# LayerNorm statistics taken by bn_stats from the transposing blocks of x, score visits gathered, timetables made anew

## The chip, the cores and the metric

The kernel runs on one core of one Trainium2 chip, in one launch, all data float32. The metric is the device time of that core in microseconds (us). The engines are named as in the profile: PE is TensorE (PEld its weight loads), DVE is VectorE, ACT is ScalarE, POOL is GpSimd, and SP is SyncE, which issues nearly all transfers.

## The reference

One layer of graph attention with residual, on 128 graphs of 128 nodes and 768 features, with 12 heads of 64:

```python
h = jnp.maximum(_layernorm(x, axis=-1), 0.0)          # mean, variance over the 768 features
q, k, v = (split_heads(h @ W + b) for W, b in ((Wq, bq), (Wk, bk), (Wv, bv)))
scores = jnp.einsum('bhqd,bhkd->bhqk', q, k) / 8 + beta * adj[:, None]
scores = jnp.where(adj[:, None] > 0, scores, -9e15)
probs = softmax(scores, axis=-1)
out = x + merge_heads(jnp.einsum('bhqk,bhkd->bhqd', probs, v))
```

x is (128, 128, 768), adj is (128, 128, 128), the three weights are 768 x 768.

## The kernel before

**Groups and products.** The work goes in 32 groups of four graphs (`NG`, `GRP`). The three matrix products h·W of a group are made by a fast scheme for matrix multiplication with fewer products. A group has three slices: `qk0` (the first half of the columns of q and k), `v`, `qk1` (the other half). A slice is 15 products (`PRODUCTS`), each of a sum of blocks of h (`A00`... loaded, `S0`... made by `sum_acts`) with a prepared sum of blocks of the weights (`T..`, `B..`). A product is 7 zones of 128 columns, written as 28 matmul records in the trace; 45 products make a group, and "slot" counts them: the times in the tables below are in slots from the group's first product. Of the 45 prepared weights ten stay in SBUF (`RESIDENT`), 35 are loaded for each group by `load_T` (448 KB each) through a ring of six.

Products add up in four chains `a` to `d`. There are four pairs of PSUM banks; a chain takes a pair at its first product in a slice (`take`) and gives it back after its last. After every product its sum so far is added to one or two of the six results of its slice (`evict`): the first time a result is written ("opened") by ScalarE with a part on VectorE, later VectorE adds from PSUM, 128 x 896 elements at a time. **The chain's next product may start only after that eviction.** When a result has all its contributions, `decode` does four (q, k) or five (v) additions within it, most of them on GpSimd.

**Attention.** For each of the six head pairs oc = 0 to 5 of a group there follow, each an event of its own: `scores` on TensorE (two halves, from decoded q and k), `mask` (VectorE: cap, add the bias, PSUM to SBUF), `exp` (ScalarE), `attend` on TensorE, `drain` (ScalarE), `recip` (VectorE), `divide` (ScalarE), `add` to the residual x (VectorE, `xo`), `send`. Attends of a group are put between the zones of a product on TensorE. Each place in TensorE's order at which one or more scores stand in a row is called a visit below; an ordinary group has four: scores (0,2) and (0,1) together, (0,0) alone, (1,2) and (1,0) together, (1,1) alone.

**Layer norm.** The products need h transposed. x is loaded in blocks (`load_x`, tile `xp`: a partition has one quarter of the features, 192, of the nodes with one remainder by 32), normalised in place by ScalarE (`norm`: relu(x·rstd + shift), one call for each 192 of a partition), and transposed by VectorE (`to_hT`). In that layout a node's features lie on four partitions, in four quarters of the 128. Groups from 2 on therefore load x a second time by rows (`load_row`, partition = node, 384 KB for a graph); ScalarE sums a row and the squares of its deviations (`row_stats`); GpSimd makes rstd and shift (`powers`); two small transfers through DRAM turn them into the block layout (`turn_out`, `turn_in`).

**The order.** Everything is written out by hand-made times. `TABLE` has an entry for each event of an ordinary group in slots, `EVICT` the delay of each eviction behind its product, `DECODE` the delay and engine of each decode, `FIRST`, `SECOND`, `LAST` what differs at the first and last groups. `put` pushes all of it into one heap; `slice_z` issues a product and then all events whose time has come. Each engine runs its instructions in that order and waits where an input isn't there:

```python
        for k, n in enumerate(order):
            outs = product(G, sl, n)
            for i, f in enumerate(outs):
                put(base + k + EVICT.get((name, n, i), 0.5), f)
            ...
            while events and events[0][0] < base + k + 1:
                _, _, f, args = heapq.heappop(events)
                f(*args)
```

Group 0 is done without the fast scheme (`plain_slice`), while the weights are prepared; group 31 ends with halved scores and attends. If the masking's bounds fail on the data, a plain version (`general`) runs after; here it doesn't.

## Time and profile before

| | |
|---|---|
| median of 3 runs | 2664.78 us (2664.27 to 2664.83) |
| span of the profiled execution | 2664.1 us |
| PE busy | 2644.1 us, 99% |
| DVE / ACT / POOL busy | 2165.8 / 1755.1 / 2097.8 us (81 / 66 / 79%) |
| granted TensorE clock | 9 of 10 or more in all 40 slices |
| moved by transfers | 736.65 MB, mean 277 GB/s |
| an ordinary group (936.60 to 1017.66) | 81.06 us |
| the first planned group (122.10 to 206.90) | 84.80 us |

The profile is one execution by the hardware's profiler. Engine shares are averages over the whole span; the order of the work repeats with each group, so a group's stretch is read instead. An engine's wait is put down to the work that ended last before it. In rows of groups the columns are line, engine, operation, written tile, read tiles and shape, with the number of instructions, then busy us and mean ns of one, then the idle time before them. Timeline rows are start, duration (us), engine, line, operation.

### The profile page before, as it was taken

How to read it: one execution, taken by the hardware profiler on the slowest of the kernel's cores; microseconds unless marked ns; L12 is line 12 of the kernel's file. 1: busy time of each engine (PE TensorE's matmuls, PEld its weight loads, DVE VectorE, ACT ScalarE, POOL GpSimd, SP SyncE). 2: the span in 40 equal slices, each digit the busy share in tenths (PEclk: the TensorE clock that was granted, in tenths of full speed). 3: DMA queues.
4: the chain of work that ended last, by engine and by line, in shares of the span. 5: the costliest groups of instructions: out<-in, count | busy, mean ns of one | idle time of the engine just before them, and what ended most of it. 6: DMA issues, size and time to landing. Idle time of an engine off the chain costs nothing.

```text
span 2664.1 us, 121442 instructions
## 1 busy us (share of the span) xinstructions
PE 2644.1 (99%) x52041; PEld 2564.2 (96%) x52041; DVE 2165.8 (81%) x2702; ACT 1755.1 (66%) x4608; POOL 2097.8 (79%) x3043
## 2 busy tenths in 40 slices
PE   9999999999999999999999999999999999999998
PEld 8799999999999999999999999999999999999997
DVE  7878887878888788887788887888877888778876
ACT  2567766677666677666777666776667776667654
POOL 5877778877779777788777797777887777887774
PEclk9999999999999999999999999999999999999999
DMA  8899999998989999999999899999899898999885
GB/s 254 276 281 279 282 284 278 283 292 267 293 281 279 287 277 284 281 281 280 289 269 288 281 281 282 288 275 285 279 278 292 268 291 279 276 286 282 256 253 165
DMA packets 531572, 736.65 MB, mean 277 GB/s; under 512 B 106444, under 2 KB 371160, under 8 KB 531032
## 3 DMA queue, kind: packets, MB, share of 16 engines
q1 hardware_dynamic: 530384, 728.06, 88.5%
q8 instruction: 411, 6.73, 1.0%
q14 instruction: 129, 1.06, 0.1%
q10 hardware_dynamic: 648, 0.79, 0.1%
HBM read 662.22 MB, written 66.51 MB: 274 GB/s over the span
## 4 chain that ended last, share of the span: by engine, by line
PE 94%; DVE 1%; DMA 0%; issue 0%; ACT 0%; SPq 0%; DVEq 0%; ACTq 0%
PE pair L681 80%; PE pair L776 7%; PE pair L855 6%; PE pair L1048 1%; DVE home L704 0%; DMA x<-in_x_dram 0%; DMA T_qk<-kept_qk 0%; PE pair L926 0%; DVE e L789 0%; DVE prep_qk L403 0%; ACT e L836 0%; DVE res_qk L403 0%; PE pair L947 0%; DVE e L931 0%; ACT e L933 0%
## 5 line engine op out<-in xcount | busy, mean ns | idle before, releaser
L704 DVE TENSOR_TENSOR home<-home,pair 128x896 f32<-128x896 f32 x836 | 880.0, 1077 | 220.5 <-PE pair L681 179.8
L681 PE MATMUL pair<-sbig,T_qk 128*64 128x128 f32 x13020 | 827.6, 274 | 2.3 <-DVE home L704 1.2
L681 PEld LDWEIGHTS pair<-sbig,T_qk 128*64 128x64 f32 x13020 | 702.5, 137 | 19.9 <-issue 12.1
L739 POOL TENSOR_TENSOR home<-home 128x256 f32<-128x256 f32 x308 | 266.1, 864 | 320.0 <-DVE home L704 319.7
L681 PE MATMUL pair<-T_v,sbig 128*64 128x128 f32 x7812 | 457.8, 273 | 1.6 <-ACT home L716 0.6
L681 PE MATMUL pair<-A,T_qk 128*64 128x128 f32 x6944 | 445.6, 273 | 0.9 <-issue 0.9
L681 PEld LDWEIGHTS pair<-T_v,sbig 128*64 128x64 f32 x7812 | 430.7, 137 | 8.4 <-ACT e L836 4.8
L855 PE MATMUL pair<-v,e 128*64 128x65 f32 x6048 | 403.5, 221 | 0.0
L836 ACT ACTIVATE e<-e,sm 128x64 f32<-128x64 f32 x1512 | 381.7, 341 | 7.4 <-DVE sm L824 6.1
L681 PEld LDWEIGHTS pair<-A,T_qk 128*64 128x64 f32 x6944 | 384.6, 137 | 1.5 <-issue 1.5
L855 PEld LDWEIGHTS pair<-v,e 128*64 128x64 f32 x6048 | 362.2, 137 | 3.2
L724 ACT ACTIVATE home<-pair 128x640 f32<-128x640 f32 x340 | 240.6, 708 | 188.5 <-PE pair L681 187.2
L681 PE MATMUL pair<-sbig,res_qk 128*64 128x128 f32 x4340 | 312.3, 273 | 0.4
L742 POOL TENSOR_TENSOR home<-home 128x256 f32<-128x256 f32 x308 | 269.7, 876 | 24.1
L885 ACT ACTIVATE sm<-pair,tiny 128x8 f32<-128x8 f32 x189 | 50.8, 269 | 329.5 <-PE pair L855 329.5
L789 DVE SCALAR_TENSOR_TENSOR e<-pair,biasT 128x1024 f32<-128x1024 f32 x189 | 229.4, 1214 | 34.1 <-PE pair L776 33.0
L740 POOL TENSOR_TENSOR home<-home 128x256 f32<-128x256 f32 x308 | 228.2, 741 | 24.1
L681 PEld LDWEIGHTS pair<-sbig,res_qk 128*64 128x64 f32 x4340 | 238.0, 137 | 1.4 <-DVE home L704 1.3
L560 ACT ACTIVATE x<-x,block 128x192 f32<-128x192 f32 x480 | 222.6, 540 | 0.0
L726 ACT ACTIVATE home<-pair,bqk 128x128 f32<-128x128 f32 x680 | 214.3, 377 | 0.0
L798 ACT ACTIVATE e<-e 128x1024 f32<-128x1024 f32 x189 | 196.1, 1055 | 21.8 <-DVE e L789 14.0
L741 POOL TENSOR_TENSOR home<-home 128x128 f32<-128x128 f32 x308 | 175.6, 570 | 24.2
(208 smaller groups left out, 4401.6 us busy)
## 6 DMA issues: line engine op xcount, KB each, us to landing
T_qk<-kept_qk SPq DMA_DIRECT2D x713, 448.0 KB
T_v<-kept_v SPq DMA_DIRECT2D x372, 448.0 KB
xo<-in_x_dram SPq DMA_DIRECT2D x190, 256.0 KB
out_dram<-xo SPq DMA_DIRECT2D x189, 256.0 KB
x<-in_x_dram SPq DMA_DIRECT2D x248, 192.0 KB
sbig<-in_x_dram SPq DMA_DIRECT2D x116, 384.0 KB
kept_qk<-prep_qk SPq DMA_DIRECT2D x23, 448.0 KB
adj<-in_adj_dram SPq DMA_DIRECT2D x128, 64.0 KB
```

The source lines that it names most:

```text
L560: nc.scalar.activation(t, t, AF.Relu, bias=shift[G, n], scale=rstd[G, n])
L681: nc.tensor.matmul(p[q:q + HD, at, :], lhs[:, q:q + HD], rhs, start=(first and at % 4 == 0), stop=True, skip_group_check=True)
L704: nc.vector.tensor_tensor(t, t, p[:, 0:7], op)
L724: nc.scalar.activation(t[:, 0:5], p[:, 0:5], AF.Copy, scale=float(sign))
L726: nc.scalar.activation(t[:, at], p[:, at], AF.Identity, bias=bqk[:, of, oc:oc + 1], scale=float(sign))
L739: e.tensor_tensor(t[:, 1:4:2], t[:, 1:4:2], twice(5), ALU.add)
L740: e.tensor_tensor(t[:, 2:5:2], t[:, 2:5:2], twice(1), ALU.add)
L742: e.tensor_tensor(t[:, 0:7:6], t[:, 0:7:6], twice(2), ALU.add)
L789: nc.vector.scalar_tensor_tensor(e[:, :, at], ps[:, :, at], SCORE_CAP * ISCALE, bias[:, :, at], op0=ALU.min, op1=ALU.add)
L798: nc.scalar.activation(e, e, AF.Exp, scale=1.0 / ISCALE)
L836: nc.scalar.activation(o[:, r, b, 0:HD], pa[:, r, b, 0:HD], AF.Copy, scale=t[:, 1, r, b:b + 1])
L855: nc.tensor.matmul(pa[q:q + HD, 2 * g + i, :], k[:, q:q + HD], vt[G, "v", r, h // 4][:, 4 * g + h % 4, :], start=True, stop=True, skip_gro ...
```

## The change

**Statistics.** From group 2 on, `load_row`, `row_stats`, `moments`, `turn_out` and `turn_in` are gone. In their place, for each half r of a group (two graphs): `bn` makes eight `bn_stats` of 128 x 192 on VectorE from the blocks that `load_x` brought; `stout` writes their 48 numbers of each partition to DRAM (192 bytes each), `stin` reads them back so that every partition has those of all four quarters (768 bytes each); `comb` joins the quarters in six small VectorE operations; `powers` makes rstd and shift in three on GpSimd.

**Order.** The product orders `ORDER`, the resident set, `TABLE`, `EVICT` and `DECODE` are new. The scores (0,2), (0,1), (0,0) stand in a row at slot 18.86, (1,2) and (1,0) at 49.99, (1,1) at 56.3: three visits a group. The program as a whole has 128 visits before and 99 now (before 67 single and 61 double; now 38 single, 32 double, 29 triple), with the same scores. Attends 1, 3 and 5 are issued whole, the others still between a product's zones (`WHOLE`). Groups 1, 2 and 31 have times of their own (`OVER`), group 0's preparation a table (`EARLY`).

**Engines.** The adds of oc 0, 1, 4, 5 and the sums S11, S10, S2 go to GpSimd (`ADD_POOL`, `SUM_POOL`); the decodes of qk0 (1,1), v (1,0) and v (1,1) come to VectorE, beside that of qk1 (0,0), which is there before too. `OPEN` lists first evictions that VectorE takes wholly (2) or for three of seven zones (1). `did` and `needs` are assertions while the program is built and issue nothing.

TensorE where the first scores of a group stand (pair is a PSUM pair, home and sbig hold results of products; L776 is a score, L681 a product). Before, two visits:

```order
L776 MATMUL pair_73<-home_154 64x128 x8
L776 MATMUL pair_73<-home_148 64x128 x8
L776 MATMUL pair_76<-home_153 64x128 x8
L776 MATMUL pair_76<-home_150 64x128 x8
L681 MATMUL pair_75<-T_v_12918,sbig 64x128 x14
L681 MATMUL pair_74<-T_v_12982,sbig 64x128 x14
L681 MATMUL pair_73<-T_v_13047,sbig 64x128 x14
L681 MATMUL pair_75<-res_v_105,A_10_11668 64x128 x14
L681 MATMUL pair_73<-T_v_13078,sbig 64x128 x14
L681 MATMUL pair_74<-T_v_13096,sbig 64x128 x14
L776 MATMUL pair_76<-home_155 64x128 x8
L776 MATMUL pair_76<-home_151 64x128 x8
```

Now (L910 is a score, L805 a product), one visit:

```order
L805 MATMUL pair_76<-T_v_14367,sbig 64x128 x14
L910 MATMUL pair_73<-home_148 64x128 x8
L910 MATMUL pair_73<-home_151 64x128 x8
L910 MATMUL pair_74<-home_154 64x128 x8
L910 MATMUL pair_74<-sbig 64x128 x8
L910 MATMUL pair_75<-home_149 64x128 x8
L910 MATMUL pair_75<-home_153 64x128 x8
L805 MATMUL pair_76<-T_v_14385,sbig 64x128 x14
```

The third score of the slice, six products later before, stands with the other two, and three PSUM pairs are filled in a row.

VectorE at the turn from one group to the next (L704 and L829 are accumulating evictions, L739 to L742 and L871 to L874 a decode, L585 and L697 sums of blocks of h, L904 and L1050 adds, L789 a mask). Before:

```order
L704 TENSOR_TENSOR sbig<-sbig,pair_76 128x896
L739 TENSOR_TENSOR home_154<-home_154 128x2x128
L740 TENSOR_TENSOR home_154<-home_154 128x2x128
L741 TENSOR_TENSOR home_154<-home_154 128x128
L742 TENSOR_TENSOR home_154<-home_154 128x2x128
L585 TENSOR_TENSOR sbig<-sbig 128x896
L904 TENSOR_TENSOR xo_1_15013<-xo_1_15013,e_1_14509 128x512
L789 SCALAR_TENSOR_TENSOR e_5_15231<-pair_74,biasT_13463 128x1024
```

Now:

```order
L829 TENSOR_TENSOR home_148<-home_148,pair_73 128x896
L871 TENSOR_TENSOR home_148<-home_148 128x2x128
L872 TENSOR_TENSOR home_148<-home_148 128x2x128
L873 TENSOR_TENSOR home_148<-home_148 128x128
L874 TENSOR_TENSOR home_148<-home_148 128x2x128
L630 TENSOR_REDUCE total_0_14041<-sbig 128x8
L631 TENSOR_SCALAR total_0_14041<-total_0_14041 128x8
L632 TENSOR_TENSOR sbig<-sbig,total_0_14041 128x64
L633 TENSOR_TENSOR sbig<-sbig 128x64
L634 SCALAR_TENSOR_TENSOR sbig<-sbig 128x64
L635 TENSOR_REDUCE total_0_14041<-sbig 128x8
L1050 TENSOR_TENSOR xo_2_13632<-xo_2_13632,e_2_13421 128x512
L697 TENSOR_TENSOR sbig<-sbig,A_11_13039 128x896
```

Between the decode and the first sum (S6 now, S0 before) stand the six operations of comb 0 and an add. On TensorE the first products of the new group stand so, and the last of these rows is the product of S6:

```order
L805 MATMUL pair_73<-A_10_11758,T_qk_12_13868 64x128 x14
L805 MATMUL pair_76<-A_11_13702,res_qk_4_102 64x128 x14
L805 MATMUL pair_75<-sbig,T_qk_1_13893 64x128 x14
L999 MATMUL pair_74<-v_101,e_1_13441 64x65 x8
L999 MATMUL pair_74<-v_96,e_1_13441 64x65 x8
L805 MATMUL pair_73<-sbig,T_qk_0_13919 64x128 x14
L805 MATMUL pair_76<-A_11_13744,T_qk_8_13955 64x128 x14
L805 MATMUL pair_75<-sbig,T_qk_5_13978 64x128 x14
```

The first row is the old group's last product; the two L999 rows are attend 1, whole, and before it no attend stood there.

The diff, cut to its core:

```diff
-ORDER = {"qk0": (1, 0, 5, 2, 10, 3, 6, 7, 13, 11, 9, 4, 14, 12, 8), "v": (1, 0, 5, 2, 10, 3, 6, 7, 13, 11, 4, 9, 14, 8, 12), "qk1": (4, 1, 0, 8, 2, 5, 3, 6, 7, 10, 9, 13, 11, 12, 14)}
+ORDER = {'qk0': (4, 1, 0, 8, 5, 2, 3, 10, 6, 7, 13, 9, 11, 12, 14), 'v': (4, 1, 8, 5, 10, 0, 3, 2, 7, 13, 6, 11, 9, 14, 12), 'qk1': (4, 3, 0, 8, 1, 7, 2, 5, 11, 6, 10, 14, 9, 13, 12)}
-RESIDENT = (10, 12, 16, 21, 29, 33, 36, 39, 41, 42)
+RESIDENT = (0, 7, 8, 9, 12, 17, 21, 30, 33, 35)
...
-    (5.399, 'sum', 'S5'), (8.41, 'sum', 'S14'), (9.857, 'sum', 'S11'), (17.129, 'scores', 0, 2),
-    (17.594, 'mask', 2), (18.011, 'exp', 2), (17.884, 'scores', 0, 1), (20.163, 'mask', 1),
+    (5.640192, 'sum', 'S5'), (9.325594, 'sum', 'S14'), (9.958879, 'sum', 'S11'), (18.858473, 'scores', 0, 2),
+    (18.861473, 'scores', 0, 1), (18.864473, 'scores', 0, 0), (19.806037, 'mask', 2), (20.078002, 'exp', 2),
...
+ADD_POOL = (0, 1, 4, 5)
+SUM_POOL = ('S11', 'S10', 'S2')
+WHOLE = (1, 3, 5)
...
+    def bn(G, g):
+        for b in range(NB):
+            nc.vector.bn_stats(st_x[:, (g % 2) * NB + b, :], xg[G, g][:, b, :])
+
+    def stout(G, r):
+        t = turned[G, r] = dram.tile([SQ, NB, 2 * NB * 6], F32, name=f"turned_{G}_{r}")
+        nc.sync.dma_start(t.rearrange("i a s -> a i s"), st_x.rearrange("p m s -> p (m s)"))
+
+    def stin(G, r):
+        nc.sync.dma_start(back.rearrange("p a m s -> p (a m s)"), turned.pop((G, r)).rearrange(
+            "i a s -> i (a s)")[None].to_broadcast([NB, SQ, NB * 2 * NB * 6]))
+
+    def comb(G, r):
+        v = back.rearrange("p a m (h s) -> p a m h s", h=2)
+        total = stat.tile([P, 2, 2 * NB], F32, tag="total", name=f"total_{G}_{r}", bufs=1)
+        nc.vector.tensor_reduce(total[:, 0], v[:, :, :, :, 1].rearrange("p a m h -> p m a h"), AX.XY, ALU.add)
+        nc.vector.tensor_scalar(total[:, 0], total[:, 0], -0.125, None, op0=ALU.mult)
+        nc.vector.tensor_tensor(dev, v[:, :, :, :, 1], total[:, 0][:, None, :, None].to_broadcast([P, NB, 2 * NB, 2]), ALU.add)
+        nc.vector.tensor_tensor(dev, dev, dev, ALU.mult)
+        nc.vector.scalar_tensor_tensor(dev, v[:, :, :, :, 2], 2.0 / QD, dev, op0=ALU.mult, op1=ALU.add)
+        nc.vector.tensor_reduce(total[:, 1], dev.rearrange("p a m h -> p m a h"), AX.XY, ALU.add)
...
-    def load_row(G, g):
-        nc.sync.dma_start(row_at(G, g), x[G * GRP + g])
-
-    def row_stats(G, g):
-        nc.scalar.activation(row, row, AF.Copy, accum_out=s[:, 0, g:g + 1])
-        nc.scalar.mul(s[:, 1, g:g + 1], s[:, 0, g:g + 1], -1.0 / D)
-        nc.scalar.activation(row, row, AF.Square, bias=s[:, 1, g:g + 1], accum_out=s[:, 2, g:g + 1])
...
+        e = nc.gpsimd if name in SUM_POOL and G > 1 else nc.vector
+        e.tensor_tensor(t, full[G, a], full[G, b], ALU.add if sign > 0 else ALU.subtract)
...
+        if (G or oc > 2) and oc in WHOLE:
+            for _ in steps:
+                pass
+        else:
+            between.append(steps)
...
-        e = nc.gpsimd if G == NG - 1 and oc < 3 else nc.vector
+        e = nc.gpsimd if oc in ADD_POOL and 0 < G < NG - 1 or G == NG - 1 and oc < 3 else nc.vector
```

More of the change, by code (lines that the diff above doesn't have):

```diff
@@ L292, in load_x @@
             home_x(G, r)
+        if G > 1:
+            for k in range(3):
+                needs("turn", *((G, f"A0{k}") if r else (1, f"A0{k}") if G == 2 else (G - 1, f"A1{k}")))
+        for _ in parts:
+            did("x", G, r)
         src = x[G * GRP + 2 * r:G * GRP + 2 * r + 2].rearrange("g (b i) (a f) -> a i (g b) f", i=SQ, a=NB)
@@ L670, in product @@
             banks[chain] = take()
+        needs("A", G, an)
+        assert not waiting.get(chain)
+        waiting[chain] = len(uses)
         bank = banks[chain]
@@ L769, in scores @@
         oc = 3 * u + j
+        if G:
+            needs("decode", G, u, j, n=2)
         ps = take()
```

443 lines of the change are left out of this document (263 added, 180 removed), and 71 rows, old and new, of tables (DECODE, EVICT, OPEN, TABLE).

## The prediction

> **What bounds the kernel now.** I read the page's head and its chain, then the stretches of a steady group, then what TensorE waited for, then its timeline around the score visits.
>
> ```profile
> span 2664.1 us, 121442 instructions
> PE 2644.1 (99%) x52041; PEld 2564.2 (96%) x52041; DVE 2165.8 (81%) x2702; ACT 1755.1 (66%) x4608; POOL 2097.8 (79%) x3043
> PE 94%; DVE 1%; DMA 0%; issue 0%; ACT 0%; SPq 0%; DVEq 0%; ACTq 0%
> ```
>
> TensorE is busy 99% of the span and is 94% of the chain that ended last. So work saved on another engine shortens nothing by itself: only TensorE's own time, or its waits, can. The profiled span is 0.7 us below the median of the runs (2664.78); I sum against 2664.1 and add 0.7 at the end.
>
> The stretches (us, busy time and count of PE, PEld, DVE, ACT, POOL, clock, DMA share, GB/s) are one steady group, and the first planned one:
>
> ```profile
> 936.60:1017.66 81.06, 81.06 (x1650) 79.45 (x1646) 66.57 (x79) 55.62 (x146) 65.48 (x95) 1.00 0.91 283
> 122.10:206.90 84.80, 81.92 (x1646) 79.37 (x1644) 67.22 (x80) 59.20 (x160) 61.50 (x89) 1.00 0.92 284
> ```
>
> A steady group is 81.06 us without an idle microsecond on TensorE, at clock 1.00. VectorE has 14.5 us to spare in it, ScalarE 25, GpSimd 15.6. What TensorE waited for (us, times, longest):
>
> ```profile
> PE pair L681 <- issue: 2.4, 6, 1.1
> PE pair L681 <- DVE home L704: 2.2, 2, 1.2
> PE pair L1048 <- ACT home L1065: 1.2, 1, 1.2
> PE pair L681 <- ACT home L716: 0.8, 2, 0.6
> PE pair L681 <- DVE e L789: 0.5, 1, 0.5
> ```
>
> These five are 7.1 us, all that new timetables could win back from waits at products. None of them is a wait for a transfer, so the second load of x is paid for nowhere on TensorE.
>
> **The change, part by part.** First TensorE. The counts of products, scores and attends stay; only the places of the scores move. Its timeline (start, length):
>
> ```profile
> 941.32 1.98 PE L776 MATMUL pair<-home 64*64 64x128 f32 x64
> ...
> 947.86 1.70 PE L681 MATMUL pair<-A,T_qk 128*64 128x128 f32 x28
> 949.49 1.10 PE L776 MATMUL pair<-home 64*64 64x128 f32 x32
> 950.52 1.97 PE L681 MATMUL pair<-sbig,T_qk 128*64 128x128 f32 x32
> ...
> 954.56 1.70 PE L681 MATMUL pair<-A,T_qk 128*64 128x128 f32 x28
> ...
> 968.66 1.70 PE L681 MATMUL pair<-T_v,sbig 128*64 128x128 f32 x28
> 970.28 1.98 PE L776 MATMUL pair<-home 64*64 64x128 f32 x64
> 972.19 4.04 PE L681 MATMUL pair<-T_v,sbig 128*64 128x128 f32 x70
> 1016.04 6.40 PE L681 MATMUL pair<-sbig,T_qk 128*64 128x128 f32 x112
> 1022.38 1.98 PE L776 MATMUL pair<-home 64*64 64x128 f32 x64
> ```
>
> The last row's start is 81.06 after the first's: the group's period. Four products from 1016.04 take 6.12 without their tail, 1.53 each. From the start of a product to the next one with one score between are 950.52 − 947.86 = 2.66, so the single visit costs 1.13; with two scores 972.19 − 968.66 = 3.53, a visit of 2.00. The second score adds 0.87; a visit has 0.26 beyond its scores. From 950.52 to 954.56 lie two products and an attend: 4.04 − 3.06 = 0.98 for the attend. The program has 128 visits before and 99 after, so **29 × 0.26 = 7.5 us** go. A triple visit isn't in the trace: if its switches cost again at each score the saving is 0, if they cost once it is 7.5. The double visit costs one 0.26, not two, so I take 7.5. Of the 7.1 us of waits I take half, **3.5**: new timetables are made for the early groups, where these waits can lie, but they move them rather than remove what causes them.
>
> Then what leaves: four row loads a group and their statistics on ScalarE.
>
> ```profile
> sbig<-in_x_dram SPq DMA_DIRECT2D x116, 384.0 KB
> SPq L543 <- DMA turned<-row: 4.2, 8, 1.0
> ```
>
> 116 × 384 KB are 45.6 MB, 1.57 a group against some 22.9 (81.06 us at 283 GB/s): the DMA share falls from 0.91 to about 0.84. Worth nothing on TensorE, since nothing waits there. Two small transfers out and two in replace one of each; the queue's wait before the one back has been at most 1.0 us, and the stream of prepared weights behind it runs six products ahead, 9 us. I cost it at nothing; were the ring empty it would be 1.0 a transfer.
>
> What arrives lands on VectorE:
>
> ```profile
> L464 DVE BATCH_NORM_STATS2 st<-x 128x6 f32<-128x192 f32 x16 | 4.4, 343 | 2.6 <-DMA x<-in_x_dram 2.6
> 67.83 0.15 DVE L478 TENSOR_REDUCE mean<-pair 128x16 f32<-128x32 f32 x1
> 68.25 0.27 DVE L481 TENSOR_TENSOR dev<-dev 128x32 f32<-128x32 f32 x1
> L904 DVE TENSOR_TENSOR xo<-xo,e x186: 674/715/1270, 126.2 to 2612.7; 128x512 f32<-128x512 f32 x186
> L904 DVE TENSOR_TENSOR xo<-xo,e 128x512 f32<-128x512 f32 x186 | 161.8, 870 | 0.1
> L585 DVE TENSOR_TENSOR sbig<-A,A 128x896 f32<-128x896 f32 x93 | 114.1, 1227 | 3.3 <-POOL A L592 3.3
> L711 DVE TENSOR_TENSOR home<-bv_b,pair 128x256 f32<-128x256 f32 x171 | 71.7, 420 | 122.1 <-PE pair L681 111.3 <-POOL home L741 7.6 <-ACT sbig L521 2.0
> L904 POOL TENSOR_TENSOR xo<-xo,e 128x512 f32<-128x512 f32 x3 | 3.6, 1185 | 9.1 <-ACT e L836 9.1
> L977 DVE TENSOR_TENSOR xo<-xo,o_last x1: 426/426/426, 2658.7 to 2658.7; 128x256 f32<-128x256 f32 x1
> L975 DVE TENSOR_TENSOR xo<-xo,o_last x3: 281/281/282, 2657.0 to 2660.3; 128x128 f32<-128x128 f32 x3
> ```
>
> Sixteen bn_stats of 0.343 are 5.5. Two combs of six small operations, each between 0.15 and 0.27, are 1.8 to 3.2; I take 2.5. Three more decodes: one is three operations of 128x256 and one of 128x128, at best 3 × 0.426 + 0.281 = 1.56, and at worst the 3.12 shown below, so 4.7 to 9.4. First evictions taken over from ScalarE (896, 640 and 384 columns, one each a group) are 2.4 by the 0.420 of 256 columns scaled up and the accumulating eviction's 1.0. Four adds leave (4 × 0.87 = 3.5) and three sums (3 × 1.23 = 3.7). From 66.6 this makes 66.6 + 5.5 + 2.5 + 2.4 − 3.5 − 3.7 + (4.7 to 9.4) = **74.5 to 79.2** in a period of 80.8. VectorE's spare time falls from 14.5 to between 1.6 and 6.3. GpSimd: 65.5 + 4 adds × 1.2 + 3 sums × 2.1 (1.185 × 896 / 512) − 3 decodes × 2.9 (below) = 67.9 and some small powers; ScalarE falls.
>
> That alone costs nothing; it costs where a result is due. The tightest place I find is the **turn from one group to the next**, where VectorE now does this:
>
> ```profile
> 1017.84 1.09 DVE L704 TENSOR_TENSOR sbig<-sbig,pair 128x896 f32<-128x896 f32 x1 [0.25 <-PE pair L681]
> 1018.84 0.65 DVE L739 TENSOR_TENSOR home<-home 128x256 f32<-128x256 f32 x1
> ...
> 1021.96 1.34 DVE L585 TENSOR_TENSOR sbig<-sbig 128x896 f32<-128x896 f32 x1
> ```
>
> The last product of the old group ends at 1016.04 + 1.53 = 1017.57; its eviction starts 0.27 later and holds VectorE 1.00, the decode 3.12 (1018.84 to 1021.96), the sum 1.34. The sum is ready at 1023.30. Its product, the fifth of the new group, comes after three products (to 1022.16), the double visit and a fourth, at 1022.16 + 2.00 + 1.53 = 1025.7: 2.4 us to spare. After the change the fifth product needs the sum S6, behind four products and an attend: 4 × 1.53 + 0.98 = 7.1 us after the old group's end. VectorE reaches S6's end after the eviction, the decode, comb 0 and an add: 0.27 + 1.00 + 3.12 + 1.25 + (0.67 to 1.27) + (1.16 to 1.27) = 7.5 to 8.2 if the decode runs as now, 5.9 to 6.6 if it runs at 1.56. So S6 lies between 0.5 early and 1.1 late, a wait of 0 to 1.1 a group. I take 0.15, between on time and the 0.3 or so of the row it is nearest to (now's decode with the short add, 7.5, less the 0.1 by which consecutive operations overlap): **29 × 0.15 = 4.4**. Behind comb 0 stand the add, S6 and S0, then the evictions of the first two products.
>
> On the price of that decode: beside the quickest add, 0.674, stand adds up to 1.270, for one shape; the excess is what meeting GpSimd's work costs. The Trainium skill, "SBUF — State Buffer", section "SBUF: two separate sides", says that a VectorE operation with two SBUF inputs and a GpSimd operation that reads SBUF exclude each other for a whole instruction, the loser blocking fully. By that the new long GpSimd operations would cost VectorE more than the rows' excess of 0.6; that is the case of blocked ports below.
>
> **Sum.** 2664.1 − 7.5 − 3.5 + 4.4 = 2657.5; with 0.7, **2658 us**.
>
> **Rivals.** *VectorE late at the turn* (slower). Decodes on VectorE stay slow and S6 comes 0.8 late in each group: 2657.5 − 4.4 + 29 × 0.8 = 2676.3, so 2677. It decides once VectorE's row of work at the turn is longer than 7.1 us by more than the visit saves, 0.26. For it: 7.5 to 8.2 above, and a second such place where the v decode now on VectorE precedes an eviction that frees a chain. Against: the adds' median of 0.715 lies near their quickest, so meetings with GpSimd are the exception.
>
> *The triple visit waits for GpSimd.* Scores stand in TensorE's order, so one late decode holds everything.
>
> ```profile
> 1012.93 1.58 POOL L739 TENSOR_TENSOR home<-home 128x256 f32<-128x256 f32 x1
> ...
> 1017.14 0.72 POOL L739 TENSOR_TENSOR home<-home 128x256 f32<-128x256 f32 x1
> ...
> 1019.29 0.79 POOL L742 TENSOR_TENSOR home<-home 128x256 f32<-128x256 f32 x1
> ```
>
> A decode takes GpSimd 2.9 (1017.14 to 1020.08) to 4.2 (1012.93 to 1017.14). From the product that completes the first of three decodes which it needs, the thirteenth of the group, to its third score are six products, three attends and two scores with their visit, 9.2 + 2.9 + 2.0 = 14.1; GpSimd must in that time wait 1.3 for the eviction and do three decodes and a 2.1 us sum: 12.1 with quick decodes, 13.4 with one slow, 16.0 with three. At 0.3 a group in place of the turn's wait: 2657.5 − 4.4 + 8.7 = 2661.8, so 2662.
>
> *Blocked ports* (slower).
>
> ```profile
> L704 DVE TENSOR_TENSOR home<-home,pair x836: 1027/1081/1091, 133.6 to 2648.4; 128x896 f32<-128x896 f32 x168
> ```
>
> If each of GpSimd's three sums of 2.1 us holds up a VectorE operation by half its length, VectorE loses 3.2 a group against 1.6 to 6.3 spare; at a wait of 0.6 a group 2657.5 − 4.4 + 17.4 = 2670.5, so 2671. Against it: the evictions, most of VectorE's work, show no spread at all (1027 to 1091), whatever GpSimd does.
>
> *The merged visit saves nothing*: 2664.
>
> **How the numbers follow.** Forecast 0.50, late turn 0.21, late triple visit 0.15, blocked ports 0.07, no saving 0.07. The forecast's own range goes from 2650 (all waits won back, none new) to 2661 (S6 0.25 late). The range is 2647 to 2678: it holds the forecast, the triple visit, blocked ports and no saving, and the lesser half of the late turn (2677 is its middle); below it would lie gains that no row shows. A measurement here tells apart about 0.2%, 5.3 us: below 2659.4 is faster, above 2670.1 slower. Faster: 0.45 of the forecast and 0.05 of the triple visit, 0.50. Same: the forecast's rest 0.05, triple visit 0.08, no saving 0.07, a short late turn 0.03, 0.23. Slower: late turn 0.18, ports 0.07, triple visit 0.02, 0.27.
>
> **What would show it.** The period from one triple visit to the next: 80.8 without waits, 80.95 as forecast, above 81.06 if the rivals hold. The triple visit 0.26 + 3 × 0.87 = 2.87 on TensorE. TensorE's waits: products for a sum would be the late turn, scores for a GpSimd decode the late triple visit, products for evictions VectorE full at another place. VectorE busy 75 to 79 a group, DMA share 0.84. The mean of the qk decode's operations on VectorE says whether 1.56 or 3.12 holds. The forecast is wrong if the waits exceed 0.26 a group, or if bn_stats costs well above 0.343 on these tiles.

## The result: 20324 us, and what the profile after shows

| | before | after |
|---|---|---|
| median, runs of one chip | 2664.81 us (2664.27 to 2665.88) | **20324.06 us** (20315.26 to 20335.22) |
| ratio | | 7.625 (7.614 to 7.636) |
| span of the profiled execution | 2664.1 us | 20313.5 us |
| of it, until the flag of the masking's bounds is made | all | 2708.7 us |

The forecast of 2658 us was wrong twice. The program does nearly all its work a second time, in its plain version; and the first pass, the work that was forecast, isn't 6 us shorter but 44.6 us longer. The page of the kernel after (busy time; the granted clock and the moved GB/s in 40 slices of the span):

```profile
PE 10549.6 (52%) x91977; PEld 9041.3 (45%) x91977; DVE 6526.6 (32%) x18408; ACT 4176.2 (21%) x13928; POOL 2889.5 (14%) x5260
PEclk9999976666666666666666666666666666666666
GB/s 253 262 262 262 259 92 26 26 26 27 26 28 26 26 26 27 28 26 26 26 26 26 27 27 26 26 26 26 28 26 26 26 26 26 28 27 26 26 26 26
```

Only the first five slices (508 us each) look like the kernel before. The timeline at the change-over:

```profile
2708.14 0.31 PE L1506 MATMUL pair<-over,ones 128*1 128x89 f32 x2 [3.56 <-DVE over L1116]
2708.50 0.23 DVE L1507 TENSOR_REDUCE bad<-pair 1x1 int32<-1x89 f32 x1
2709.55 0.20 POOL masks.py:197 MEMSET g_ident<- 128x128 f32 x1 [8.23 <-DVE bad L1507]
```

`bad` collects whether a sum of exponentials left its bounds. With it set, `general` starts: every later instruction works on tiles named `g_`. That is 17.6 ms.

**Why the flag is set** is read in the code, and the first experiment bears it out. `st_x`, into which `bn` writes, lies inside the tile that still holds x of group 1's second half. For group 2 the table of exceptions has

```python
    (2, 'bn', 1): 37.0592, ...      # in OVER
    (37.1557, 'turn', 1, 'A11'), ...
```

so `bn` of group 2's second graph writes its 24 numbers a partition just before `A11` of group 1 is transposed out of the same columns. One graph of group 1 then gets columns of sums in place of normalised x, and the flag rises. `stin` asserts that the turns `A1k` have been; `bn` does not.

**The first pass.** Two groups of the kernel after, a steady one and the first planned one (us, then PE, PEld, DVE, ACT, POOL, clock, DMA share, GB/s), and what TensorE waited for until 2710:

```profile
952.10:1034.70 82.60, 81.21 (x1649) 79.55 (x1647) 74.14 (x117) 45.46 (x125) 69.27 (x92) 1.00 0.90 262
121.40:210.20 88.80, 84.18 (x1647) 81.17 (x1644) 75.44 (x118) 47.80 (x134) 64.08 (x91) 0.98 0.83 251
```

```profile
PE pair L805 <- ACT home L856: 18.1, 28, 0.7
PE pair L805 <- issue: 10.4, 14, 1.8
PE pair L805 <- ACT home L842: 9.6, 9, 2.7
```

A steady group takes 82.60 against 81.06 before, the first 88.80 against 84.80. TensorE's waits come in three kinds, each with its place.

The forecast's own two places first, in the timeline of that steady group (the group begins at 952.12):

```profile
953.46 0.81 DVE L871 TENSOR_TENSOR home<-home 128x256 f32<-128x256 f32 x1
...
955.97 0.27 DVE L630 TENSOR_REDUCE total<-sbig 128x8 f32<-128x64 f32 x1
...
957.29 0.22 DVE L635 TENSOR_REDUCE total<-sbig 128x8 f32<-128x64 f32 x1
...
957.43 0.68 DVE L1050 TENSOR_TENSOR xo<-xo,e 128x512 f32<-128x512 f32 x1
...
958.03 1.08 DVE L697 TENSOR_TENSOR sbig<-sbig,A 128x896 f32<-128x896 f32 x1
958.25 2.36 POOL L647 TENSOR_TENSOR rstd<-total,nhalf 128x8 f32<-128x8 f32 x1
...
959.21 1.75 PE L805 MATMUL pair<-sbig,T_qk 128*64 128x128 f32 x28
...
960.93 2.74 ACT L661 ACTIVATE x<-x,shift,rstd 128x192 f32<-128x192 f32 x6 [2.93 <-POOL shift L648]
...
963.58 2.01 ACT L974 ACTIVATE e<-e,sm 128x64 f32<-128x64 f32 x8
...
966.07 0.61 ACT L856 ACTIVATE home<-pair,bqk 128x128 f32<-128x128 f32 x2
...
966.73 1.75 PE L805 MATMUL pair<-sbig,res_qk 128*64 128x128 f32 x28 [0.66 <-ACT home L856]
```

The decode is 2.51 (953.46 to 955.97), comb 1.5 (to 957.51), the sum S6 is ready at 959.11 and its product starts at 959.21: on time. What is late stands 7 us further on: comb, the power on GpSimd (2.36 for 128 x 8 numbers), six norms on ScalarE, a divide, and only then the first eviction (L856) for which the next product of chain a waits, 0.66 here. This is the 18.1 us row.

```profile
987.64 1.70 PE L805 MATMUL pair<-T_v,sbig 128*64 128x128 f32 x28
989.27 1.54 PE L910 MATMUL pair<-home 64*64 64x128 f32 x48
990.63 0.62 PE L910 MATMUL pair<-sbig 64*64 64x128 f32 x16
991.07 1.05 PE L910 MATMUL pair<-home 64*64 64x128 f32 x32
992.05 1.20 PE L805 MATMUL pair<-T_v,sbig 128*64 128x128 f32 x18
```

The triple visit: product to product 992.05 − 987.64 = 4.41, less 1.53 for the product, is 2.88. The forecast said 2.87.

The row of 9.6 us (`ACT home L842`), at its longest, further on in the kernel after. SPq issues transfers, L606 is bn, L837 an eviction's part on VectorE, L841 and L842 the rest of it on ScalarE:

```profile
2217.68 5.72 SPq L533 DMA_DIRECT2D T_v<-kept_v  x4
...
2220.82 0.42 DVE L837 TENSOR_TENSOR home<-bv_b,pair 128x256 f32<-128x256 f32 x1 [0.51 <-PE pair L805]
...
2224.50 1.14 DVE L606 BATCH_NORM_STATS2 sbig<-x 128x6 f32<-128x192 f32 x4 [3.26 <-DMA x<-in_x_dram]
...
2225.55 0.73 DVE L837 TENSOR_TENSOR home<-bv_b,pair 128x256 f32<-128x256 f32 x2
2225.99 0.60 ACT L841 ACTIVATE home<-pair 128x512 f32<-128x512 f32 x1 [3.95 <-DVE home L837]
...
2226.48 0.27 ACT L842 ACTIVATE home<-pair 128x128 f32<-128x128 f32 x1
...
2226.80 1.52 PE L805 MATMUL pair<-res_v,A 128*64 128x128 f32 x22 [2.71 <-ACT home L842]
```

Read from the bottom: the product waits 2.71 for ScalarE, which waits 3.95 for VectorE, which has stood 3.26 at its first bn because x hadn't landed. Everything queued behind bn on VectorE stands with it. At all 9 places of this row, a bn that had itself waited at least 0.25 us stands in the 6 us before. Over the steady groups (busy, mean ns, then the idle time before bn; and what SyncE's queue waited for):

```profile
L606 DVE BATCH_NORM_STATS2 sbig<-x 128x6 f32<-128x192 f32 x456 | 126.5, 342 | 32.2 <-DMA x<-in_x_dram 24.0 <-DMA T_qk<-kept_qk 4.4 <-DMA T_v<-kept_v 2.0
```

```profile
SPq L620 <- DMA turned<-sbig: 94.4, 53, 3.2
SPq L612 <- DVE sbig L606: 73.4, 28, 4.4
```

The third kind, `issue`, is TensorE waiting for nothing the profile names. In the trace's transfer records most of them end 1.3 to 1.7 us after a packet of 16 KB has landed on the queue marked "instruction" (q8): some 15 us at 18 places of the first pass, worked out from the starts of TensorE's instructions, against some 3 us at 8 places before. That is a coincidence in time; that TensorE waits for what the packet holds is not shown.

### The profile page after: what moved, and what is told of

It reads as the page before. It is cut to its first block, busy times and chain, and to the rows that moved or that the text cites. A ratio compares the mean times of both kernels' runs of the same rounds, so it can differ in the third digit from the quotient of the medians.

```text
span 20313.5 us, 288774 instructions
## 1 busy us (share of the span) xinstructions
PE 10549.6 (52%) x91977; PEld 9041.3 (45%) x91977; DVE 6526.6 (32%) x18408; ACT 4176.2 (21%) x13928; POOL 2889.5 (14%) x5260
## 5 line engine op out<-in xcount | busy, mean ns | idle before, releaser
L1571 PE MATMUL g_pt<-g_ident,g_xn 128*128 128x128 f32 x4608 | 1977.9, 429 | 7923.1 <-DVE g_xn L1567 7640.8
L1571 PEld LDWEIGHTS g_pt<-g_ident,g_xn 128*128 128x128 f32 x4608 | 919.4, 200 | 8462.4 <-issue 7752.4
L1572 ACT ACTIVATE g_hT<-g_pt 128x128 f32<-128x128 f32 x4608 | 1279.1, 278 | 11057.7 <-PE g_pt L1571 11057.7
L1577 PE MATMUL g_pv<-g_wv,g_hT 128*128 128x128 f32 x9216 | 2648.1, 385 | 0.0
L1577 PEld LDWEIGHTS g_pv<-g_wv,g_hT 128*128 128x128 f32 x9216 | 2348.7, 310 | 49.3
L1580 PE MATMUL g_pq<-g_hT,g_wq 128*128 128x128 f32 x9216 | 2233.4, 349 | 0.0
L1580 PEld LDWEIGHTS g_pq<-g_hT,g_wq 128*128 128x128 f32 x9216 | 1935.3, 268 | 0.0
L1580 PE MATMUL g_pk<-g_hT,g_wk 128*128 128x128 f32 x9216 | 1154.6, 275 | 0.0
L1606 PE MATMUL g_pa<-g_v,g_pT 128*128 128x64 f32 x3072 | 847.5, 367 | 546.0 <-ACT g_pT L1604 546.0
L1580 PEld LDWEIGHTS g_pk<-g_hT,g_wk 128*128 128x128 f32 x9216 | 1090.8, 192 | 0.0
L805 PE MATMUL pair<-sbig,T_qk 128*64 128x128 f32 x14756 | 897.8, 273 | 15.5 <-issue 9.8
L829 DVE TENSOR_TENSOR home<-home,pair 128x896 f32<-128x896 f32 x824 | 870.5, 1077 | 97.5 <-PE pair L805 90.6
L805 PEld LDWEIGHTS pair<-sbig,T_qk 128*64 128x64 f32 x14756 | 818.7, 137 | 27.8 <-issue 18.3
```

Of the source, the lines that this page charges most:

```text
L805: nc.tensor.matmul(p[q:q + HD, at, :], lhs[:, q:q + HD], rhs, start=(first and at % 4 == 0), stop=True, skip_group_check=True)
L829: nc.vector.tensor_tensor(t, t, p[:, 0:7], op)
L1571: nc.tensor.transpose(pt, xn[:, c * P:(c + 1) * P], ident)
L1572: nc.scalar.activation(hT[:, c, :], pt, AF.Relu)
L1577: nc.tensor.matmul(pv, hT[:, c, :], w_sb["wv"][:, c, :], start=(c == 0), stop=(c == NC - 1))
L1580: nc.tensor.matmul(p, w_sb[name][:, c, :], hT[:, c, :], start=(c == 0), stop=(c == NC - 1))
```

## The experiments

Each time is compared with the kernel before on the same chip, at 2664.8 to 2669.3 us; a time without a range is one run. All kernels from here on, but for the two made from the kernel before, have the first edit.

**1. The flag.** `bn` of group 2's second graph goes behind group 1's last turn, nothing else.

```diff
-    (2, 'bn', 1): 37.0592, ...
+    (2, 'bn', 1): 37.17, ...
```

> The changed kernel with one number of its timetable for group 2 moved: bn of the second graph stands behind the three transposes of group 1's second half (slot 37.17) instead of ahead of the last of them (37.06). Theory: bn writes its 24 numbers into memory that still holds x of one graph of group 1, the results of that graph grow beyond the bound, and the flag sends the program through its plain second version. Then the second pass goes, and the time is that of the first pass in the profile of the changed kernel, which ended at 2708.7: 2709 to 2711. Rival: the new statistics themselves, or another place, set the flag; then it stays at some 20320.

Measured 2713.26 us (2710.21 to 2714.89) against 2666.34: ratio 1.0173 (1.0153 to 1.0193). The overwritten columns cost 17.6 ms; the other loss stays whole. This "corrected kernel" is the object of the rest. Its waits are those of the first pass (17.5, 10.1 and 8.1 us for the same three rows).

**2. The wait at chain a, one operation at a time.** ScalarE's divide 1 goes behind the first eviction, in two strengths; or comb goes ahead of the decode on VectorE.

```diff
-    (49.436934, 'divide', 1)        # experiment a: 50.55; experiment b: 51.2
-    (-45.382883, 'comb', 0)         # experiment c: -45.8
```

> As the first run of this call, and on ScalarE the first eviction of product 5 of qk0 stands ahead of divide 1 instead of behind it. Theory of the first pass's lost time: at the turn of a group the chain comb 0 (VectorE), powers (GpSimd, 3.3 us), norm and divide 1 (ScalarE) ends 0.79 us too late for that eviction, for which product 10 of its chain waits, in each of 29 groups, 22.9 us. Divide 1 takes 2.0 us, so the wait should vanish: 2710 - 23 = 2687. Rival: VectorE is full, at 74.3 of 81 us a group, and the wait turns up at the next product: 2705 to 2710.

> As the first corrected kernel, and divide 1 stands on ScalarE behind the first evictions of both product 5 and product 2 of qk0. Where it stood behind product 5's alone, the wait of product 10 (22.1 us in 28 groups) was gone, and one of 10.1 us had come at product 6, which needs product 2's eviction. Theory: it is the order on ScalarE behind the late norm, nothing else; then this wait goes too, 2705 - 10 = 2695. Rival: the norm's lateness passes on to the next eviction or to the transposes, and it stays at 2700 to 2705.

> As the first run of this call, and comb 0 stands ahead of the decode of qk1 (0,0) on VectorE instead of behind it, 2.5 us earlier; the sum S6 behind both is where it was. If the chain through comb 0 and powers is what holds product 10, its wait goes as in the run before, 2687, though divide 1 is left where it was. If it is only the order on ScalarE, or VectorE's fullness, nothing changes, 2710. A new wait for the score that needs the moved decode would show as a wait of a score for VectorE.

Measured 2705.07 (a), 2714.18 (b; ratio 1.0176, 1.0159 to 1.0193) and 2718.71 (c): a at its rival's figure, b and c slower than even theirs. TensorE's longest group of waits for a result in b, then in c:

```profile
PE pair L805 <- ACT home L842: 12.7, 8, 2.3
PE pair L805 <- DVE home L829: 11.3, 23, 0.9
```

```profile
PE pair L805 <- DVE e L924: 16.6, 31, 0.7
```

The wait of 18 us for L856 falls to 6.3 in a, 0.6 in b and 1.9 in c, and in b and c one of 11 to 17 us for VectorE stands a few products away.

**3. bn or the turns at another place on VectorE.** bn 2 later; the turns A00 to A02 behind an eviction (with b); both.

```diff
-    (-28.956387, 'bn', 2)           # d: -28.4;  f: -27.5
-    (-38.307544, 'turn', 'A00'), (-38.053772, 'turn', 'A01'), (-36.36296, 'turn', 'A02')
+    (-35.6400, 'turn', 'A00'), (-35.6395, 'turn', 'A01'), (-35.6390, 'turn', 'A02')   # e and f
```

> As the first run of this call, and bn of the third graph stands behind the first evictions of products 4 and 1 of v on VectorE instead of between them. Theory: bn waits there for x to land (27 times, 24.0 us in the profile of the changed kernel) and the first evictions behind it are late for product 8 of v (11 waits, 8.7 us): 2710 - 9 = 2701. Rival: the wait for x only moves to the evictions behind bn's new place and costs as much: 2710.

> As the run with divide 1 behind both evictions, where a wait of 17.6 us had come at product 9 of qk0, which needs VectorE's eviction of product 6, and the three transposes of the group's first half stand behind that eviction on VectorE instead of ahead of it. Theory: the transposes wait for norm (about 1 us, 28.1 us in all in the profile of the changed kernel) and hold the eviction behind them; then the wait goes: 2714 - 17 = 2697. Rival: what is late there moves on to the next eviction, of product 7, or to the inner sums on GpSimd: 2705 to 2714.

> As the run before in this call, and bn of the third graph stands behind the decode of qk0 (1,1) on VectorE, which the triple visit needs, so that its wait for x stands neither ahead of first evictions nor of that decode. Theory: the waits at product 8 of v (7 to 11 us) go and the triple visit doesn't wait as it did with bn ahead of the decode (2735): about 2688 if the run before gives 2697. Rival: bn and the transfers behind it then end late, and comb 1, powers and norm hold the second half's transposes: no gain or a loss, 2697 to 2710.

Measured 2735.56 (d), 2723.21 (e) and 2725.64 (f; ratio 1.0213, 1.0196 to 1.0230). All slower than the corrected kernel. In d, scores now wait for VectorE:

```profile
PE pair L910 <- DVE sm L962: 9.3, 28, 0.9
```

I had read each wait as a fault of one place in the table. Six moves, and each time other waits came: that reading falls. Nor does the time follow bn's wait for x. In the corrected kernel that wait is 21.4 us between 210 and 2600; in d, then in f, it is

```profile
DVE sbig L606 <- DMA x<-in_x_dram: 13.3, 10, 2.2
```

```profile
DVE sbig L606 <- DMA x<-in_x_dram: 4.7, 7, 1.2
```

and both are slower. In e, from which f differs by bn 2's place alone, it is 43.9: 39 us less of it in f, and the time is 2 us longer.

**4. The visits.** The kernel of b, with the third score of the triple visit alone again, some five products later.

```diff
-    (18.864473, 'scores', 0, 0)
+    (23.44, 'scores', 0, 0)
```

> As the run with divide 1 behind both evictions, and the score (0,0) stands alone at slot 23.44 again instead of in one visit with the two others: four visits a group. If a visit costs 0.26 us beyond its scores, the time rises by 29 x 0.26 = 7.5 over that run, and the stretch from the product ahead of the double visit to the one behind it is 3.53 and of the single 2.66 us, as in the kernel before. If three scores in a row hold up work elsewhere (three pairs of PSUM taken at once), the time falls instead.

Measured 2730.63, one run, 16 above b instead of 7.5. Two new waits, some 9 and 8 us by the products' starts, stand at two products of the slice v; it seems that the long visit had also given the evictions time between two products of a chain. So the merged visit is worth its 0.26 a group and, in this timetable, some 9 us besides (b's own runs lie up to 5 apart).

**5. Without any statistics.** bn, the small transfers, comb and the power are out, so mean and variance of x are not computed from group 2 on; then, in that kernel, the four loads of x of each half two slots apart instead of close together. The second edit, for the first half (the other half likewise):

```diff
-    (-56.236887, 'load_x', 0, (0,)), (-55.556421, 'load_x', 0, (2,)), (-54.398256, 'load_x', 0, (3,)), (-54.23248, 'load_x', 0, (1,)),
+    (-56.236887, 'load_x', 0, (0,)), (-54.0, 'load_x', 0, (2,)), (-51.8, 'load_x', 0, (3,)), (-49.6, 'load_x', 0, (1,)),
```

> As the first corrected kernel, but from group 2 on the statistics are left out: no bn, no transfers out and back, no comb, no powers; norm takes 0 and 1 in their place, so layer norm is not computed there (left out of the computation: mean and variance). This prices the whole new path. Theory: the waits of products 10 of qk0 (22), 8 of v (7) and of attends and products behind bn go, and TensorE's waits for instructions (14) fall if the small transfers cause them: 2713 - 29 = 2684 without the last, 2672 with it. Rival: the new timetable itself loses the time, and it stays above 2700. A period of 80.8 us would show the three visits' saving.

> As the kernel without statistics from group 2 on (2679), and the four loads of x of each half stand 2.2 slots apart instead of in a burst. In that kernel TensorE waited 14 us in 20 places about 1.4 us behind the landing of a 16 KB block on the queue of instructions, the kernel before 3 us in 8 places. Theory: these blocks queue behind the burst of x loads and land late; spread, the waits fall by half or more: 2679 - 7 = 2672. Rival: other transfers, or the density of TensorE's instructions, cause them, and it stays at 2676 to 2682.

Measured 2679.01, and with the loads apart 2663.72. Undisturbed groups take 80.80 us in both, the period that the forecast gave for a group without waits. Waits put down to `issue` at products, close together, then apart:

```profile
PE pair L808 <- issue: 7.6, 15, 1.4
```

```profile
PE pair L808 <- issue: 3.6, 8, 0.8
```

Places that follow a landed instruction packet go from 20 to 11 (14.0 to 7.3 us). That is somewhat less than half of the 15 us. As much again is the clock: with the loads close together the granted clock is 0.50 for 3.4 us at four places (from 22.0, 161.9, 2636.6 and 2663.9 us), a loss of 1.7 each; with the loads apart it is 1.00 there. Three of the four places lie ahead of the first moved load or behind the last, so some 5 of the 15 us are not the loads' doing.

The same in the whole corrected kernel, one slot apart, and the reverse in the kernel before, with its four loads in one burst:

> The corrected kernel, whole, with the four loads of x of each half one slot apart (1 us and more) instead of two close pairs. Theory (the burst of x delays the blocks of instructions that TensorE runs next): TensorE's waits put down to issue fall from 10 us to about 5, and 2713 becomes 2700 to 2708. Rival: the moments of x on VectorE wait longer for the later loads and give it back: 2710 to 2720.

> The kernel before, whole, with the four loads of x of each half issued in one burst at the place of the first. Theory (a burst of x delays TensorE's blocks of instructions in any kernel): waits put down to issue rise from 3 us, and 2665 becomes 2670 to 2680. Rival (the delay needs the other order's places): 2663 to 2668.

Measured 2746.51, against 2669.28 for the kernel before in those runs, and 2673.50. In the corrected kernel spreading costs 33 us instead of winning 5 to 13, a miss of both expectations: bn now waits for x 75.6 us in all, and SyncE behind it.

```profile
DVE sbig L606 <- DMA x<-in_x_dram: 75.6, 40, 6.2
```

```profile
SPq L612 <- DVE sbig L606: 142.8, 31, 6.2
```

So bn ties the table down: x must be there when VectorE gets to it. A burst in the kernel before gives `issue` 5.9 us at products instead of 2.4 and 4 us more in one run, little more than runs differ; that a burst alone is dear isn't shown.

**6. The second load of x, out of the kernel before.** Row loads, row statistics and their transfers are left out of the kernel before.

> The kernel before, with its statistics left out from group 2 on: no loads of rows, no sums on ScalarE, no moments, powers and small transfers; norm takes 0 and 1 (mean and variance are left out of the computation). Theory of the prediction: what the change removes was hidden entirely, since nothing on TensorE waited for it: 2664, within 3 us. Rival: the 46 MB slow other transfers or instruction fetches, and their going is worth some us: 2655 to 2661.

Measured 2659.81, one run, against 2668.17 of the kernel before in those runs (2666.22 to 2672.50), spans 2658.0 and 2664.1: 6 to 8 us. What the change removes was not free.

**7. Load or bond?** Is VectorE too busy, or does somebody wait for the chain of statistics? First the norm doesn't wait (it takes constants), all work kept. Then GpSimd's power doesn't wait for comb either.

```diff
         # norm, groups 2 on: bias and scale from constant tiles
-        needs("comb", G, r)
-        total = ve_of.pop((G, r))
+        total = stat.tile([P, 2, 2 * NB], F32, tag="loose", ...)     # power: reads a tile of ones
```

> As the first corrected kernel with all its instructions, but from group 2 on norm takes 0 and 1 instead of the statistics' results (layer norm's mean and variance are not applied there), so that norm no longer waits for comb 0 and powers. All of VectorE's and GpSimd's work and all transfers are kept. Theory: the lateness of this chain makes the wait at the turn of the groups; then product 10's wait of 22 us goes and no other comes, 2713 - 22 = 2691, and with the waits behind bn kept it is well above the 2679 of the kernel without statistics. Rival: VectorE's load of 74 us a group makes the waits, wherever the timetable leaves least room; then it stays at 2705 to 2715.

> The corrected kernel with all work of the statistics kept (bn, the small transfers, comb, the power), but with both bonds behind comb loosed: the power on GpSimd reads a tile of constants and doesn't wait for comb, and the norm takes shift 0 and scale 1 (mean and variance of x are not applied). Theory (GpSimd, which serves in order, stands waiting for comb ahead of its power, and that is the loss): first reading near the run without bn and comb, 2667 us, so 2665 to 2680. Rival (VectorE's own load is the loss): it stays at 2705 to 2722, as with the norm alone unbound (2720).

Measured 2720.32 and 2710.02 (ratio 1.0157, 1.0140 to 1.0174). With all work kept and neither norm nor power bound to comb, nothing clear of noise is won: it isn't the bonds behind comb. Those ahead of it stay: bn waits for x, and SyncE's transfer out waits for bn. Then the load in parts. Without bn and comb on VectorE (power and transfers kept; SyncE has no bn to wait for):

> The corrected kernel with the statistics' share of VectorE left out: no moments of x (bn) and no combination (comb), so VectorE loses about 40 + 6 short operations a group; the power and its neighbours stay on GpSimd (on a tile of constants), and the small transfers that turn the sums stay too. The norm takes shift 0 and scale 1, so mean and variance of x are not applied. Theory (VectorE's added work makes the waits): first reading near that of the kernel without any statistics, 2679 us, so 2680 to 2692. Rival (GpSimd's power and the small transfers on SyncE make them): it stays at 2708 to 2722, as with the norm unbound (2720).

Measured **2666.91**, against 2669.28 for the kernel before. Without comb alone:

> The same, and comb left out as well (bn on VectorE, the small transfers and the power on GpSimd stay; mean and variance of x are not applied). If the run with both bonds loosed stays above 2700: theory that comb's 1.5 us on VectorE at the start of a group is the loss gives 2665 to 2685; rival that bn's 40 short operations a group and its waits for x are the loss gives 2695 to 2715. If that run falls to 2680 or less, this one lies within 8 us below it.

Measured 2717.48 (ratio 1.0189, 1.0172 to 1.0207). So comb is worth nothing here, and **bn, with all that hangs on it, is worth some 50 us** (2717.48 − 2666.91, the second one run on another chip). The expectations count 40 short operations of bn a group; there are 16. What TensorE waited for, and the stretch from 210 to 2600 (columns as above), without comb:

```profile
PE pair L802 <- ACT home L839: 26.9, 16, 3.2
```

```profile
210.00:2600.00 2390.00, 2345.82 (x47459) 2303.99 (x47457) 2084.79 (x3001) 1310.85 (x3574) 1945.79 (x2632) 1.00 0.88 260
```

and without bn and comb:

```profile
PE pair L802 <- issue: 9.9, 12, 1.8
```

```profile
210.00:2600.00 2390.00, 2377.64 (x48437) 2341.94 (x48435) 2002.48 (x2585) 1339.41 (x3650) 1989.96 (x2670) 1.00 0.90 264
```

With bn in, TensorE is busy 32 us less in the same 2390 us, and its largest wait is that of the chain shown above (x late, bn, eviction, product): at all 16 places a bn that had waited at least 0.25 us stands in the 6 us before. Without bn that wait is gone altogether, and `issue` is the largest. Some 11 us more of the difference are the clock: by the traces' clock records it is at half for 27.9 us of the whole run with bn, and for 5.0 us without.

**What about bn costs this is not separated.** It brings 5.4 us of work a group to VectorE, its own wait for x, and SyncE's wait for it; the run without bn drops all three. The wait for x alone doesn't explain it: in experiments d and f it was shorter and the time longer, and in the corrected kernel the chain's row is only 8.1 us. VectorE's load as a sum doesn't either: without comb VectorE is busy 2084.79 us of the 2390 instead of 2161.39 with both bonds loosed, and nothing is won. And in experiment 8, where SyncE never waits for bn, bn still waits 33.1 us for x. A bn on data that are already there was not tried.

**8. A counter-test that told something else.** Power and small transfers out, bn and comb kept.

> The counterpart: bn and comb stay on VectorE, but the power on GpSimd and the small transfers that turn the sums (out to the tile in rows and back) are left out; the norm takes shift 0 and scale 1, so mean and variance of x are not applied. Theory (VectorE's added work makes the waits): it stays at 2708 to 2722. Rival (GpSimd and the transfers make them): 2679 to 2692. A result between, near 2695 to 2705, says that both have a share.

Measured 2793.99, outside both expectations. GpSimd, freed of the power, does its add nearly 5 us earlier in the group, beside VectorE's:

```profile
813.02 1.10 DVE L1048 TENSOR_TENSOR xo<-xo,e 128x512 f32<-128x512 f32 x1
813.53 1.62 POOL L1048 TENSOR_TENSOR xo<-xo,e 128x512 f32<-128x512 f32 x1
814.05 2.06 DVE L695 TENSOR_TENSOR sbig<-sbig,A 128x896 f32<-128x896 f32 x1
...
816.21 2.19 PE L803 MATMUL pair<-sbig,T_qk 128*64 128x128 f32 x18 [2.27 <-issue]
```

VectorE's add takes 1.10 and S6 2.06, against 0.68 and 1.08 in the kernel after, where GpSimd is at its power meanwhile. S6's product waits in 28 of 29 groups, 2.7 us on average (74.6 in all, worked out from the products' starts). That is the forecast's rival of blocked ports, at a place of its own. The Trainium skill, "SBUF — State Buffer", section "SBUF: two separate sides", says that such pairs of operations exclude each other; a doubling of VectorE's time agrees with it. Evictions, which read one operand from PSUM, stay at 1.08 on average here as in the kernel after; the forecast's evidence against this rival, their even times, was no evidence on sums with both operands in SBUF. For the question it was made for, the run tells little.

## Why the prediction was wrong, step by step

- **That the change does what it says** was taken for granted, and no rival held the contrary. The text on the change names group 2's own times (`OVER`); where `bn` writes, and who reads those columns last, was not followed. This step cost 17.6 ms.
- **29 × 0.26 for the visits:** right. 2.88 against 2.87, 80.80 in groups without waits.
- **Half of the 7.1 us of waits won back (−3.5):** wrong in sign. `issue` alone went from 2.4 to 10.4 at products, and the first planned group from 84.80 to 88.80 (1.7 of the 4.0 are 3.4 us at half clock). The list of five waits is a selection: three longer ones, of 3.6, 2.0 and 1.5 us at the program's start and end, are not in it.
- **S6 at the turn (+4.4):** near. The decode took 2.51, between the 1.56 and 3.12 given; S6's product waited 6 times, 2.7 us in all (by the products' starts). It was not the place that mattered.
- **"Sixteen bn_stats of 0.343 are 5.5 … That alone costs nothing":** the step that failed for the first pass. The price is right (0.342), and VectorE's load nearly (74.14 against 74.5 to 79.2). But the row quoted for the price had `2.6 <-DMA x<-in_x_dram` at its end: this operation waits for its data, on an engine that serves in order. I named what stands behind comb 0 and never what stands behind bn. With what hangs on it, bn measured about 50 us, 1.7 a group, in place of 0; how much of that is this wait is open (experiment 7).
- **"Behind comb 0 stand the add, S6 and S0":** the other path out of comb (power, norms, ScalarE's first evictions) was left out; it is the 18.1 us row. In the runs with the bonds loosed that row goes and the time stays, so it is where the loss came out, not its cause.
- **The second load of x "worth nothing on TensorE":** wrong, by the one run; 6 to 8 us, though no wait for it stood in TensorE's list.
- **Small transfers, at most 1.0 each:** they measured 94.4 / 53 = 1.8 on SyncE's queue, and SyncE waited another 73.4 / 28 = 2.6 each for bn. None of TensorE's waits in the first pass is put down to a transfer, so it paid nothing directly. That these waits delay the loads of x behind them, and so the next bn, fits the rows; but in experiment 8, which has neither, bn waits for x no less (33.1 us against 21.4 in the corrected kernel).
- **DMA share 0.84:** wrong. The rate fell about as worked out (283 to 262 GB/s), the busy share only from 0.91 to 0.90; why a byte became dearer is open.

The sum with measured terms: 2664.1 − 7.5 (visits) = 2656.6; the run without bn and comb has a span of 2665.1, so all the rest, gains and losses, makes 8.5, of which more `issue` waits are the part that can be read; bn and comb add 46 (2713.3 − 2666.9, the corrected kernel against that run): 2711. That this is the span of the corrected kernel (2711.4) proves nothing, as the last two terms are differences of measured times; about 8 of the 46 are the clock, at half for 21.0 us against 5.0.

Of the rivals, "VectorE late at the turn" named the right engine and sign, at 2677, but the wrong place. That the run without any statistics (2679) is slower than the one without bn and comb alone (2667) is for 7 of the 12 us the clock, at half for 18.8 us against 5.0; the rest is open. No version that computes all beat the kernel before.

## What to carry to other kernels

Spare time on an engine doesn't make work moved to it free: an operation there can wait for a transfer, and it holds up everything queued behind it. So look at what it waits for and at what waits behind it, and price it by a run that leaves it out; here short operations that fitted into the spare time cost some 50 us, and their wait for data alone does not account for it. Where every engine is written out in order and little slack is left, moving one operation moves the wait; only taking work away removed it. And when a change writes into a tile shared in time, list who reads those columns last, also for the first and last rounds whose times are exceptions.

## What the runs showed of the hardware

**The clock falls after short pauses.** The plain version goes six times over the 128 graphs. In each of these 768 rounds TensorE stands about 10 us (row below), and the granted clock is 0.65 from 3000 to 20000.

```profile
10007.84 0.45 PE L1571 MATMUL g_pt<-g_ident,g_xn 128*128 128x128 f32 x1 [9.95 <-DVE g_xn L1567]
```

In experiment 8 a pause of 2.3 us is sometimes enough. The stretch behind it, and the next one:

```profile
816.20:820.00 3.80, 3.79 (x48) 3.47 (x52) 3.55 (x4) 0.16 (x1) 3.13 (x4) 0.55 0.38 127
820.00:830.00 10.00, 10.00 (x214) 9.83 (x208) 9.24 (x10) 6.27 (x19) 5.80 (x6) 1.00 0.89 236
```

For 3.8 us the clock is 0.55, so the wait costs 1.7 us more than itself; behind another such pause (1073 us) it stayed at 1.00. The Trainium skill, "TensorE: Matmul & The Clock Gate", Part 1, gives an idle window of about 3.4 us for the fall; here less sufficed, at some of the pauses.

**Blocks of instructions may come late.** Most of TensorE's waits for `issue` end 1.3 to 1.7 us behind a 16 KB packet on the queue marked "instruction", at 18 places of the first pass. The Trainium skill, "Runtime: NRT & Kernel Launch", section "Instruction fetch mechanics", calls crossing such a block mostly hidden. If these waits are such crossings, they cost up to 1.8 us at a place and 10 to 15 us in all here, with transfers busy 0.90 of the time.

**GpSimd's power** of 128 x 8 numbers takes 2.36 us, as long as two of its additions of 128 x 512; the prediction had it as "some small powers".
